# A graph-attention layer on one core: scores from f16 planes on half arrays, tiles in pair order, 46 of 48 tiles turned by DMA

## The chip, the core and the metric

The kernel runs on one core of one Trainium2 chip, in one launch. The metric is device time in microseconds, the median of the runs. TensorE (PE) multiplies; its weight loads are listed apart as PEld. VectorE (DVE), ScalarE (ACT) and GpSimd (POOL) do elementwise work. SyncE (SP) issues most transfers, and 16 DMA engines carry them out.

## The reference, cut to what matters

```
h = relu(layernorm(x))                       # x: 384 x 1024
q, k, v = h @ wq.T + bq, h @ wk.T + bk, h @ wv.T + bv
q2 = (q @ wiq.T + biq)  -> 16 heads x 384 x 64      # the same for k2 (wik), v2 (wiv)
scores = q2 @ k2.T / 8 + mask                # per head, 384 x 384
attn = softmax(scores)
out = x + (attn @ v2) @ wo.T + bo
```

The mask is -inf but for the edges of a graph (6,528 edges, softplus weights by edge type) and the diagonal. All is float32. Some biases and weights are scaled up, so that a plain f16 product is not exact enough: the kernel writes a float32 operand as a high and a low part and adds three products (high x high, high x low, low x high).

## The kernel before, in words

Weights come in 56 chunks of 128 x 1024 (`chunks`): 8 each of v, q, iv, k, then iq and ik alternately for 8 pairs of heads, then 8 of o. A chunk is loaded on SP into one of four `raw` buffers five chunks ahead (`load`, L80), and split two chunks ahead into a high part on ScalarE (`split_hi`, L102 or L108) and a low part on VectorE or GpSimd (`split_lo`, L125 and L127; in the tile loop in halves, L118, or quarters, L113). A chunk of a projection is 8 groups of three matmuls (`mm3`, L459 to L461) with 384 columns.

The iv, iq, o and k weights are scaled by a power of two and split into f16; v, q and ik stay fp32r. A scale comes from a bound: the weight chunks are read once more as "scans" (L140), ScalarE sums absolute values along each row (`scan_sum`, L146), and `bound` turns the column of row sums on TensorE (L167) and takes a maximum and a power of two (`power`, L149 to L152). There are scans for iv, k, iq and o, 8 each. The bounds are made at the chunk numbers in `BOUNDS`.

The v and q projections, the iv and the k projection fill chunks 0 to 31. Then iq and ik follow for 8 pairs of heads, from chunk 32 (`W0`) on. Their matmuls are the filler of a loop over 48 tiles: a generator gives 3 matmuls at a time (`fill_qk`), and later the output projection gives 3 matmuls of 512 columns at a time, charged 4 (`fill_o`). `PRE` = 84 of the 384 filler matmuls are done ahead of the loop, then `RATE` = 7.9 in each step. The chunks of wo are split at the steps in `WSTEPS` and released three steps later (`wready`).

A tile is 128 rows of one head's scores; before, tile i is head i // 3 and row block i % 3. `now[0]` is the step. The work of tile i stands in these steps:

- step i, `do_S` (L927, L928): two fp32r matmuls on 128 rows, since q and k of one head are stacked: rows 0 to 63 the high and 64 to 127 the low part of q, both against the high part of k; then q against a second operand (`kz`) that holds the low part of k in one half and zeros in the other. The stacks are copied together by DMA, four copies of 96 KB per operand (`qk_done`, L777), mostly on SP.
- step i + 1, `do_ttr` (L936): VectorE adds the mask and takes the row minimum (the signs are turned).
- step i + 2, `do_exp` (L941): ScalarE takes the exponential and the row sum.
- step i + 3, `do_recip` (L961, L964): reciprocals.
- 27 tiles (`in_dma`) are scaled and split into f16 planes by `do_high` (L976, ScalarE) and `do_low` (L980, VectorE) and turned by a DMA transpose on SP (`do_turn`, L984). The other 21 are scaled on GpSimd (`do_norm`, L968), turned by three fp32 transposes on TensorE (`turn_mm`, L990) and split out of PSUM by `do_pt` (L997 on ScalarE, L998 on VectorE).
- three steps after a pair's last turn, `av_mm` (L1008): 18 matmuls per pair of heads, 64 columns each, the two heads in the two halves of the columns. `do_ao` (L1013) and `do_aos` (L1016, L1017) write the result for the output projection.

The order on each queue is the order in which the loop calls these. PSUM has eight banks of 512 columns: three `g` for the filler, two `s` for scores, two `t` for transposes, one `a` for attention. At the end come the last wo chunk for six output blocks and the stores (`finish`, L877 and L1099).

Of the kernel before, what the change touches and what calls it, by code (L numbers as in the profile page):

```python
# [27 lines left out]
def gnn_kernel(ctx: ExitStack, tc: tile.TileContext, x, edges, erows, etw, wq, wk, wv, wiq, wik, wiv, wo,  # L28
# [15 lines left out]
    EB = 6  # L44
# [5 lines left out]
    def bank(tag):  # L50
        return psum.tile([128, 512], F32, tag=tag, name=tag, bufs={"g": 3, "a": 1}.get(tag, 2))
# [30 lines left out]
    def weight_scale(w):  # L82
        return {"iv": u_iv, "iq": u_iq, "o": u_o, "k": u_k}.get(chunks[w][0])
# [46 lines left out]
    SCANS = sorted([(n, i + c, i + c + g, i) for n, c, g in (("iv", 3, 2), ("k", 11, 2), ("iq", 18, 2), ("o", 25, 2)) for i in range(8)], key=lambda c: c[1])  # L130
    SROW = {"iv": 1, "k": 2, "iq": 1, "o": 2}

    def scan_buf(i):
        first = sum(c[1] < 25 for c in SCANS)
        return scan[:, i % 3, :] if i < first else qF3[:, (i - first) % 3, :]
# [6 lines left out]
    def scan_sum(w):  # L142
        for i, (n, _, at, k) in enumerate(SCANS):
            if at == w:
                x = scan_buf(i)
                nc.scalar.activation(x, x, AF.Abs, accum_out=l1[:, SROW[n], k:k + 1])  # L146

    def power(t, u, src):
        nc.vector.tensor_reduce(t, src, axis=AX.X, op=OP.max)  # L149
        nc.vector.tensor_scalar(t.bitcast(I32), t.bitcast(I32), 0x7F800000, None, op0=OP.bitwise_and)  # L150
# [3 lines left out]
    BOUNDS = {8: 0, 13: 1, 17: 2, 21: 5, 29: 3, 37: 4}  # L154

    def bound_of(w):
        return ((0, t_v, u_v), (1, t_iv, u_iv), (0, t_q, u_q), (1, t_iq, u_iq), (2, t_o, u_o), (2, t_k, u_k))[BOUNDS[w]]

    def bound_max(w):
        if w in BOUNDS:  # L160
            i, t, _ = bound_of(w)
            nc.vector.tensor_reduce(t, l1[:, i, :], axis=AX.X, op=OP.max)

    def bound(w):
        _, t, u = bound_of(w)
        ps = bank("g")
        nc.tensor.transpose(ps[:, :128], t.to_broadcast([128, 128]), ident)  # L167
        power(t, u, ps[:, :128])
# [27 lines left out]
    small = const.tile([128, 57], F32, name="small")  # L196
# [5 lines left out]
    t_k, u_k, s_k = (small[:, c:c + 1] for c in (13, 14, 15))  # L202
    l1 = const.tile([128, 3, 8], F32, name="l1")
# [132 lines left out]
    rrow = work.tile([128, 2, N], F32R, tag="qs", name="rrow").bitcast(F32)[:, 0, :]  # L336
# [21 lines left out]
    def ln_row():  # L358

        ps = bank("t")  # L360
# [13 lines left out]
    def ln_transpose(t):  # L374
        pss = []
        for half in range(2):
            ps = bank("st"[half] if t < 2 else "ga"[half])
# [108 lines left out]
    def evac_f(ps, dst, m, bias):  # L486
# [3 lines left out]
        nc.scalar.activation(f, dst[:, m, :], AF.Abs, accum_out=l1[:, 0, m:m + 1])  # L490
# [16 lines left out]
    def slot_head(w):  # L507
# [3 lines left out]
        if w > 17:  # L511
            planes_of(w - 18, qT, qF, u_q)
# [11 lines left out]
    def bounds(w):  # L524
        if w in BOUNDS:
            bound(w)
        if w == 21:
            nc.vector.tensor_scalar(s_k, t_k, 1.0 / HSC, None, op0=OP.mult)  # L528
        if w == 29:
            nc.vector.tensor_tensor(u_c, u_q, u_iq, OP.mult)  # L530
            nc.vector.tensor_scalar(bias_q, bc[:, 24:32], u_c, None, op0=OP.mult)
            nc.vector.scalar_tensor_tensor(neg_c, t_q, -0.125, t_iq, op0=OP.mult, op1=OP.mult)
# [33 lines left out]
    hk = []  # L566
    for j in range(2):
        t = work.tile([128, 2, N], F32R, tag="nat", name="hk", bufs=2).bitcast(F16)
        hk += [t.rearrange("p a n -> p (a n)").rearrange("p (k a n) -> p k a n", k=2, a=2)[:, k, :, :] for k in range(2)]
    t = work.tile([128, 2, 2, N], F32R, tag="kz", name="hkz", bufs=1).bitcast(F16)  # L570
    hk += [t.rearrange("p a b n -> p (a b n)").rearrange("p (k a n) -> p k a n", k=4, a=2)[:, k, :, :] for k in range(4)]
# [37 lines left out]
    def residual(k):  # L609

        if k == 0:
            for j in range(2):
                t = work.tile([128, 2, N], F32R, tag="ks", name="bot")
                bob[j] = t.bitcast(F32).rearrange("p k n -> p (k n)")[:, 0:512]
# [36 lines left out]
    _, vF, vT = staged("g2")  # L651
# [5 lines left out]
    accs = [bank("ststag"[i]) for i in range(6)]  # L657
# [16 lines left out]
    def v2_early():  # L674
        t = work.tile([128, 2, N], F32R, tag="qs", name="tv")
        tv = t.bitcast(F32).rearrange("p a n -> p (a n)")[:, :512]
# [24 lines left out]
    def o_scale():  # L701
        _, t, u = bound_of(W0 + 5)
# [36 lines left out]
    kz = work.tile([128, 2, 2, N], F32R, tag="kz", name="kz", bufs=1)  # L739
    for j in range(2):  # L740
        nc.gpsimd.memset(kz.bitcast(F32)[64 * j:64 * j + 64, :, 1 - j, :], 0.0)

# [3 lines left out]
    issues = []  # L746
    stacks = {}
    gps = {}

    def qk_done(w):  # L750
        n, p = chunks[w]
        q2 = nc.scalar if p == 0 else nc.sync
        if n == "iq":
            nat = work.tile([128, 2, N], F32R, tag="nat", name="nat", bufs=2)
            evac(gps[w], nat[:, 0, :], nat[:, 1, :], bias_q[:, p:p + 1])
            nf = nat.bitcast(F32)
            qs = work.tile([128, 2, N], F32R, tag="qs", name="qs")
            qf = qs.bitcast(F32)
            copies = [(nc.sync, qf[0:64, 0, :], nf[0:64, 0, :]), (q2, qf[64:128, 0, :], nf[0:64, 1, :]),
                      (nc.sync, qf[0:64, 1, :], nf[64:128, 1, :]), (q2, qf[64:128, 1, :], nf[64:128, 0, :])]  # L760
            stacks["q", p] = qs
        else:
            kh = work.tile([128, 2, N], F32R, tag="nat", name="nat", bufs=2)[:, 0, :]
            kl = kz[:, p % 2]
            evac(gps[w], kh, None, bc[:, 32 + p:33 + p])
            for o in range(2):
                r = slice(o * 64, o * 64 + 64)
                soon(1, lambda r=r, o=o, ps=gps[w]: nc.vector.scalar_tensor_tensor(  # L768
                    kl[r, o, :], ps[r, :N], bc[r, 32 + p:33 + p], kh.bitcast(F32)[r, :], op0=OP.add, op1=OP.subtract))
            nf = kh.bitcast(F32)  # L770
            ks = work.tile([128, 2, N], F32R, tag="ks", name="ks")
            kf = ks.bitcast(F32)
            copies = [(q2 if r else nc.sync, kf[r * 64:(r + 1) * 64, o, :], nf[o * 64:(o + 1) * 64, :])
                      for o in range(2) for r in range(2)]
            stacks["k", p] = ks, kl
        for q, a, b in copies:
            issue = lambda q=q, a=a, b=b: q.dma_start(a, b)  # L777
            if q is nc.scalar:
                issues.append(issue)
            else:  # L780
                after(issue)
# [13 lines left out]
    def qk_head(w):  # L795
        if pendq:
            pendq.pop(0)()
        if 0 < w - W0 < NTAB:
            mask_select(w - W0)
        split_hi(w + 2, None, False, 2 if w + 2 < WO else 1)  # L800
        while issues:
            issues.pop(0)()
# [10 lines left out]
        load(w + 5)  # L813
        scan_load(w)
        scan_sum(w)
        if w == W0:
            mask_select(0)
        if w == W0 + NTAB - 1:
            mask_scale()
        bound_max(w)  # L820
        if w == W0 + 6:
            o_scale()

    def fill_qk():
        nonlocal w
        for p in range(8):
            for n in ("iq", "ik"):
# [5 lines left out]
                for k in range(KT):  # L833
                    colmm(gps[w], w, src, k)
                    yield 3
# [9 lines left out]
    PRE, RATE, RATE_O, RATE_E = 84, 7.9, 8, 8  # L845
    WSTEPS = (35, 37, 41, 44, 47, 51)
# [72 lines left out]
    S = 48  # L919

    def do_S(i):
# [5 lines left out]
        nc.tensor.matmul(ps[:, :N], qs[:, o, c], ks[:, o, :], start=True, stop=False)  # L927
        nc.tensor.matmul(ps[:, :N], qs[:, o, c], kl[:, o, :], start=False, stop=True)  # L928

    def do_ttr(i):  # L930
        t = i % 3
        e = es[i] = work.tile([128, N], F32, tag="e", name="e", bufs=EB)
        if t == 0:
            sts[i // 3] = work.tile([128, 9], F32, tag="s", name="s", bufs=4)
        s = sts[i // 3]
        nc.vector.tensor_tensor_reduce(e, st_ps.pop(i)[:, :N], ma[:, t, :], neg_c, 3.0e38, OP.add, OP.min, s[:, t:t + 1])  # L936

    def do_exp(i):
        h, t = divmod(i, 3)
        s = sts[h]  # L940
        nc.scalar.activation(es[i], es[i], AF.Exp, bias=s[:, t:t + 1], scale=-1.0, accum_out=s[:, 3 + t:4 + t])  # L941

    ptv, plv = [], []

    XP = 1

    def pt_setup():
# [3 lines left out]
        f = ptv.pop()  # L951
        plv.extend(f[:, 2 * j:2 * j + 2, :] for j in range(3))
        plv.extend(work.tile([128, 2, N], F16, tag="pl", name="pl", bufs=XP) for _ in range(XP))

    def factor(i):
        return sts[i // 3][:, 6 + i % 3:7 + i % 3]

    def do_recip(i):
        s = sts[i // 3]
        a, b = (0, 2) if i % 3 == 1 else (2, 3)  # L960
        nc.vector.reciprocal(s[:, 6 + a:6 + b], s[:, 3 + a:3 + b])  # L961
        b = min(b, 1 + in_dma(i // 3 * 3 + 1))
        if a == 0:
# [184 lines left out]
```

## Time and profile before

| what | us |
|---|---|
| runs | 282.38 (281.54 to 287.32) |
| profiled execution, its own time | 282.02 |
| its span, first to last instruction | 280.3 |
| TensorE busy in the span | 273.9 |
| VectorE busy | 230.6 |
| ScalarE busy | 210.6 |
| first score matmul starts | 156.5 |
| last score matmul of a tile begins | 253.4 |

The span is what the trace holds; the kernel's own time is 1.7 us longer. Busy time is the union over an engine's instructions. A matmul's duration in the timeline is a latency: the next starts before it ends, so the distance between starts is what one costs TensorE.

### The profile page before, as it was taken

Reading aid. Unit: us, or ns where it says so; the run is one execution under the profiler, and the core shown is the slowest. Engines: PE = TensorE matmul, PEld = TensorE weight load, DVE = VectorE, ACT = ScalarE, POOL = GpSimd, SP = SyncE. Lnnn points to the kernel's source line nnn. Section 1 sums busy time; section 2 is a strip of 40 time slices with the busy share of each in tenths; the row PEclk is TensorE's granted clock in tenths of the full one; section 3 lists DMA queues with packets and bytes.
Section 4 is the critical chain, followed back from the end, with each engine's and each line's share of the span. In section 5 each row is a group of like instructions: output and inputs, shape, how many; then the busy total and the mean of one; then the engine's idle time right before and its main releaser. Section 6 shows DMA issues by size and latency. Waiting matters only on the chain. (4 is left out here: it accounts for less than half of the span.)

```text
span 280.3 us, 5120 instructions
## 1 busy us (share of the span) xinstructions
PE 273.9 (98%) x1631; PEld 204.0 (73%) x1631; DVE 230.6 (82%) x545; ACT 210.6 (75%) x417; POOL 146.4 (52%) x170
## 2 busy tenths in 40 slices
PE   7999999999999999999999999999999999999994
PEld 6899999999954444666677887878878695655443
DVE  4858986999998956978998987897988889999423
ACT  3796778599896927989795877688888897777510
POOL 3755656456678754659953443547373632332310
PEclk9999999999999999999999999999999999999999
DMA  7899999999987987688897699999999989432105
GB/s 254 275 303 403 383 397 381 323 302 411 348 284 258 345 289 251 238 285 321 279 329 270 173 278 257 202 199 190 213 210 197 235 218 259 108 67 48 37 12 215
DMA packets 46859, 70.42 MB, mean 251 GB/s; under 512 B 26736, under 2 KB 32368, under 8 KB 46832
## 3 DMA queue, kind: packets, MB, share of 16 engines
q1 hardware_dynamic: 44448, 67.90, 78.4%
q0 software_dynamic: 2064, 1.80, 2.4%
q10 hardware_dynamic: 320, 0.39, 0.6%
q8 instruction: 13, 0.21, 0.3%
q14 instruction: 14, 0.11, 0.1%
HBM read 55.08 MB, written 3.39 MB: 209 GB/s over the span
## 5 line engine op out<-in xcount | busy, mean ns | idle before, releaser
L459 PE MATMUL g<-g,whl 128*128 128x384 f32 (+1 forms) x248 | 83.8, 338 | 0.0
L316 POOL DMA_INDIRECT tab<-edge x51 | 61.7, 1210 | 40.8 <-DMA tab<-edge 27.2
L461 PE MATMUL g<-g,whl 128*128 128x384 f32 (+1 forms) x248 | 82.5, 333 | 0.0
L460 PE MATMUL g<-g,whl 128*128 128x384 f32 (+1 forms) x248 | 82.4, 332 | 0.0
L102 ACT ACTIVATE whl<-raw,small 128x1024 f16<-128x1024 f32 (+1 forms) x36 | 34.8, 971 | 7.9 <-DVE small L528 5.3
L125 DVE SCALAR_TENSOR_TENSOR whl<-raw,small,whl 128x1024 f16<-128x1024 f32 x24 | 32.4, 1350 | 6.4 <-ACT whl L102 6.4
L459 PEld LDWEIGHTS g<-g,whl 128*128 128x128 f32 x184 | 34.6, 188 | 0.3
L460 PEld LDWEIGHTS g<-g,whl 128*128 128x128 f32 x184 | 34.6, 188 | 0.0
L461 PEld LDWEIGHTS g<-g,whl 128*128 128x128 f32 x184 | 34.5, 188 | 0.0
L936 DVE CUSTOM_DVE_ANT_0 e<-s,ma,small 128x384 f32<-128x384 f32 x48 | 29.0, 606 | 1.7 <-PE s L928 1.4
L941 ACT ACTIVATE e<-e,s 128x384 f32<-128x384 f32 x48 | 29.1, 607 | 0.8 <-DVE s L936 0.6
L108 ACT ACTIVATE whl<-raw 128x1024 fp32r<-128x1024 f32 (+1 forms) x30 | 25.2, 848 | 1.4 <-DMA raw<-in_wv_dram 1.4
L976 ACT ACTIVATE pt<-e,s 128x384 f16<-128x384 f32 x21 | 12.9, 613 | 17.4 <-POOL s L964 17.4
L146 ACT ACTIVATE scan<-scan 128x1024 f32<-128x1024 f32 x23 | 24.0, 1044 | 0.0
L968 POOL TENSOR_TENSOR e<-e,s 128x384 f32<-128x384 f32 x21 | 17.3, 825 | 12.1 <-DVE s L961 8.2
L113 POOL TENSOR_TENSOR whl<-raw,whl 128x256 fp32r<-128x256 f32 x20 | 18.1, 912 | 8.7 <-ACT whl L108 8.7
L927 PE MATMUL s<-ks,qs 128*128 128x384 f32 x48 | 20.8, 433 | 0.7 <-DMA ks<-nat 0.3
L127 DVE TENSOR_TENSOR whl<-raw,whl 128x1024 fp32r<-128x1024 f32 x15 | 19.4, 1293 | 2.4 <-ACT whl L108 2.3
L459 PEld LDWEIGHTS <-whl 128*128 128x128 f16 x128 | 12.5, 97 | 11.0 <-issue 4.4
L1017 POOL TENSOR_TENSOR g<-aof,g 128x384 f16<-128x384 f32 x8 | 7.4, 923 | 23.8 <-ACT g L1016 23.8
L461 PEld LDWEIGHTS <-whl 128*128 128x128 f16 x128 | 12.5, 98 | 8.2
L980 DVE SCALAR_TENSOR_TENSOR pt<-e,s,pt 128x384 f16<-128x384 f32 x21 | 15.7, 749 | 3.3 <-ACT pt L976 3.3
(197 smaller groups left out, 642.7 us busy)
## 6 DMA issues: line engine op xcount, KB each, us to landing
raw<-in_wv_dram SPq DMA_DIRECT2D x8, 512.0 KB, 7.1
raw<-in_wq_dram SPq DMA_DIRECT2D x8, 512.0 KB, 6.3
scan<-in_wiv_dram SPq DMA_DIRECT2D x8, 512.0 KB, 7.2
raw<-in_wiv_dram SPq DMA_DIRECT2D x8, 512.0 KB, 5.6
scan<-in_wk_dram SPq DMA_DIRECT2D x8, 512.0 KB, 6.3
raw<-in_wk_dram SPq DMA_DIRECT2D x8, 512.0 KB, 4.7
g<-in_wo_dram SPq DMA_DIRECT2D x8, 512.0 KB, 5.8
raw<-in_wiq_dram SPq DMA_DIRECT2D x8, 512.0 KB, 4.8
```

What stands on the lines that cost most here:

```text
L102: soon(j if parts > 1 else -1, lambda c=c: nc.scalar.activation(hi[:, c], raw[w][:, c], AF.Copy, scale=sc))
L108: soon(j if parts > 1 else -1, lambda c=c: nc.scalar.activation(hi[:, c], raw[w][:, c], AF.Copy))
L125: nc.vector.scalar_tensor_tensor(lo, raw[w], sc, hi, op0=OP.mult, op1=OP.subtract)
L127: (eng or nc.vector).tensor_tensor(lo, raw[w], hi.bitcast(F32), OP.subtract)
L146: nc.scalar.activation(x, x, AF.Abs, accum_out=l1[:, SROW[n], k:k + 1])
L316: nc.gpsimd.indirect_dma_start(out=tabs[c // RNG], out_offset=bass.IndirectOffsetOnAxis(ap=idx[:, c:c + 1], axis=0), in_=val[:, c:c + 1], ...
L459: nc.tensor.matmul(ps, lhi, rhi, start=first, stop=False)
L460: nc.tensor.matmul(ps, lhi, rlo, start=False, stop=False)
L461: nc.tensor.matmul(ps, llo, rhi, start=False, stop=last)
L927: nc.tensor.matmul(ps[:, :N], qs[:, o, c], ks[:, o, :], start=True, stop=False)
L936: nc.vector.tensor_tensor_reduce(e, st_ps.pop(i)[:, :N], ma[:, t, :], neg_c, 3.0e38, OP.add, OP.min, s[:, t:t + 1])
L941: nc.scalar.activation(es[i], es[i], AF.Exp, bias=s[:, t:t + 1], scale=-1.0, accum_out=s[:, 3 + t:4 + t])
```

## The change

The iq and ik results are no longer stacked. Both are scaled to f16 planes (high and low), q by norms of the operands through the weight's own scale, k by a scale applied when it leaves PSUM. For that there are scans of ik too (40 scans in place of 32), the scans of k, iq and ik sum squares, and the scales come from square roots of the sums (`root_power`, `score_scale`). Four of the o scans are reduced on VectorE. Some scans have only one slot between load and sum, and there is a third place for their buffers.

A score tile is now three f16 matmuls (the terms high x high, low x high, high x low), each on 64 rows of the array: the even head of a pair has rows 0 to 63, the odd head rows 64 to 127. Tiles go in the order of the pairs: pair i // 6, row block, then the two heads; `do_S` does both heads in one step of two. `s` has four banks, `t` none, `a` one. All tiles but the last two are turned by DMA. The filler is paced by a planned length of a step, `STEP`, less what scores, attention and transposes are charged. `do_aos` writes its high part on VectorE. Weight loads in the loop are issued two steps later (`LD`).

```diff
-    EB = 6
+    EB = 8
...
-        return psum.tile([128, 512], F32, tag=tag, name=tag, bufs={"g": 3, "a": 1}.get(tag, 2))
+        return psum.tile([128, 512], F32, tag=tag, name=tag, bufs={"g": 3, "s": 4}.get(tag, 1))
...
-        return {"iv": u_iv, "iq": u_iq, "o": u_o, "k": u_k}.get(chunks[w][0])
+        return {"iv": u_iv, "iq": u_w, "o": u_o, "k": u_k}.get(chunks[w][0])
...
-    SCANS = sorted([(n, i + c, i + c + g, i) for n, c, g in (("iv", 3, 2), ("k", 11, 2), ("iq", 18, 2), ("o", 25, 2)) for i in range(8)], key=lambda c: c[1])
-    SROW = {"iv": 1, "k": 2, "iq": 1, "o": 2}
+    SCANS = [("iv", i + 3, i + 5, i) for i in range(8)] + [("k", i + 11, i + 13, i) for i in range(8)]
+    SCANS += [("iq", i + 16, i + 18, i) for i in range(8)]
+    SCANS += [("ik", i + 23, i + 25 - (i > 3), i) for i in range(8)] + [("o", i + 27, i + 27 + 2, i) for i in range(8)]
+    SCANS.sort(key=lambda c: c[1])
+    SROW = {"iv": 1, "k": 2, "iq": 1, "ik": 2, "o": 1}
+
+    def home(n, at):
+        return 2 if at > 24 else 1 if n == "iq" and 16 <= at < 22 else 0
...
-                nc.scalar.activation(x, x, AF.Abs, accum_out=l1[:, SROW[n], k:k + 1])
+                if n == "o" and w < 33:
+                    nc.vector.tensor_reduce(l1[:, SROW[n], k:k + 1], x, axis=AX.X, op=OP.max, apply_absolute_value=True)
+                    continue
+                nc.scalar.activation(x, x, AF.Square if n in ("k", "iq", "ik") else AF.Abs,
+                                     accum_out=l1[:, SROW[n], k:k + 1])
...
+    def root_power(t, u, src):
+        nc.vector.tensor_reduce(t, src, axis=AX.X, op=OP.add)
+        nc.vector.tensor_scalar(t.bitcast(I32), t.bitcast(I32), 1, 0x7F800000, op0=OP.logical_shift_right,
+                                op1=OP.bitwise_and)
+        nc.vector.tensor_scalar(t, t, 2.0 ** -104, 2.0 ** 50, op0=OP.max, op1=OP.mult)
+        nc.vector.reciprocal(u, t)
...
+    def bias_max():
+        ps = bank("g")
+        for i in range(3):
+            nc.tensor.transpose(ps[:, i * 128:i * 128 + 128], bmax[:, i:i + 1].to_broadcast([128, 128]), ident)
...
+    def score_scale(t, u, i, bias):
+        nc.vector.tensor_tensor(t, t, bmax[:, i:i + 1], OP.add)
+        exponent(t)
+        nc.vector.tensor_scalar(t, t, 2.0 ** -14, 2.0 ** -50, op0=OP.mult, op1=OP.max)
+        nc.vector.reciprocal(u, t)
+        nc.vector.tensor_scalar(bias, bc[:, 16 + 8 * i:24 + 8 * i], u, None, op0=OP.mult)
...
     def qk_done(w):
         n, p = chunks[w]
+        pl = qk[n, p] = work.tile([128, 2, N], F16, tag="qp" if n == "iq" else "kp", name=n, bufs=3)
+        hi, lo = pl[:, 0, :], pl[:, 1, :]
+        ps, b = gps[w][:, :N], (bias_q if n == "iq" else bias_k)[:, p:p + 1]
         if n == "iq":
...
+            nc.scalar.activation(hi, ps, AF.Identity, bias=b)
+            after(lambda: nc.vector.scalar_tensor_tensor(lo, ps, b, hi, op0=OP.add, op1=OP.subtract))
         else:
...
+            f = work.tile([128, 512], F32, tag="aof", name="f", bufs=3)[:, :N]
+            nc.scalar.activation(f, ps, AF.Identity, bias=b, scale=u_k2)
+            after(lambda: nc.vector.tensor_copy(hi, f))
+            after(lambda: (nc.gpsimd if p else nc.vector).tensor_tensor(lo, f, hi, OP.subtract))
...
-        load(w + 5)
+        soon(LD, lambda: load(w + 5))
...
-    PRE, RATE, RATE_O, RATE_E = 84, 7.9, 8, 8
-    WSTEPS = (35, 37, 41, 44, 47, 51)
+    PRE, STEP, UNIT, SMM, AMM = 90, 1.96, 0.168, 0.7, 1.69
+    WSTEPS = (36,38,41,44,47,51)
+    LD = 2
...
     def in_dma(i):
-        h, t = divmod(i, 3)
-        return t == 0 or t == 1 and (h < 10 or h == 14)
+        return i < S - 2
+
+    def tile_of(i):
+        p, r = divmod(i, 6)
+        return p, r // 2, r % 2
...
     def do_S(i):
-        h, t = divmod(i, 3)
-        p, o = divmod(h, 2)
-        qs, (ks, kl) = stacks["q", p], stacks["k", p]
-        ps = st_ps[i] = bank("s")
-        c = slice(t * 128, (t + 1) * 128)
-        nc.tensor.matmul(ps[:, :N], qs[:, o, c], ks[:, o, :], start=True, stop=False)
-        nc.tensor.matmul(ps[:, :N], qs[:, o, c], kl[:, o, :], start=False, stop=True)
+        p, t, _ = tile_of(i)
+        q, k = qk["iq", p], qk["ik", p]
+        pair = [bank("s") for _ in range(2)]
+        for j, (a, b) in enumerate(TERMS):
+            for o in range(2):
+                r = slice(o * 64, o * 64 + 64)
+                nc.tensor.matmul(pair[o][:, :N], q[r, a, t * 128:(t + 1) * 128], k[r, b, :], start=(j == 0), stop=(j == 2))
+        st_ps[i], st_ps[i + 1] = pair
...
-        nc.scalar.activation(ao[:, 0, p, :], aof[p], AF.Copy)
+        nc.vector.tensor_copy(ao[:, 0, p, :], aof[p])
...
+    LAGH, LAGL, LAGT = (5, 5), (6, 6), (6, 6)
...
+    t_at = {i + 5: i for i in range(S) if not in_dma(i)}
+    a_at = {6 * p + 14 if p < 7 else 54: p for p in range(8)}
     for i in range(S + 12):
         now[0] = i
-        r = RATE if len(gens) == 2 else RATE_O if i < S else RATE_E
+        scores = i < S and i % 2 == 0
+        r = (STEP - SMM * scores - AMM * (i in a_at) - 0.33 * (i in t_at)) / UNIT
         fill(r / 2)
-        if i < S:
+        if scores:
             do_S(i)
         fill(r / 2)
```

More of the change, by code (lines that the diff above doesn't have):

```diff
@@ L202, in gnn_kernel @@
     t_k, u_k, s_k = (small[:, c:c + 1] for c in (13, 14, 15))
+    bias_k, bmax = small[:, 57:65], small[:, 65:68]
+    t_ik, u_ik, t_q2, u_q2, t_k2, u_k2, u_q7, u_w = (small[:, c:c + 1] for c in range(68, 76))
     l1 = const.tile([128, 3, 8], F32, name="l1")
@@ L335, in gnn_kernel @@
     var = lnt[:, 1:2 * NT:2]
[L336 removed]
+    rrow = work.tile([128, N], F32, tag="qp", name="rrow", bufs=3)
     def ln_bn(t, h):
@@ L376, in ln_transpose @@
         for half in range(2):
-            ps = bank("st"[half] if t < 2 else "ga"[half])
+            ps = bank("s" if t < 2 else "ga"[half])
             for j in range(4):
@@ L564, in proj @@
             w += 1
[L566 to L571, printed above, removed]
+    hk = [work.tile([128, 2, N], F16, tag="pl" if k < 5 else "kp", name="hk", bufs=5 if k < 5 else 3)
+          for k in range(KT)]
     hs = {}
@@ L655, in gnn_kernel @@
     proj(hT, qF, 0, extra_q)
-    accs = [bank("ststag"[i]) for i in range(6)]
+    accs = [bank("ssssag"[i]) for i in range(6)]
     for k in range(8):
@@ L674, in v2_early @@
     def v2_early():
-        t = work.tile([128, 2, N], F32R, tag="qs", name="tv")
-        tv = t.bitcast(F32).rearrange("p a n -> p (a n)")[:, :512]
+        tv = work.tile([128, 512], F32, tag="aof", name="tv", bufs=3)
         nc.scalar.activation(tv, accs[5], AF.Copy)
@@ L738, in gnn_kernel @@
     flush(True)
-    kz = work.tile([128, 2, 2, N], F32R, tag="kz", name="kz", bufs=1)
-    for j in range(2):
-        nc.gpsimd.memset(kz.bitcast(F32)[64 * j:64 * j + 64, :, 1 - j, :], 0.0)
     ao = gtile("g1").bitcast(F16).rearrange("p a k n -> p (a k n)")[:, :2 * KT * N]
     ao = ao.rearrange("p (a k n) -> p a k n", a=2, k=KT)
-    issues = []
-    stacks = {}
+    qk = {}
     gps = {}
@@ L834, in fill_qk @@
                     colmm(gps[w], w, src, k)
+                    if k == 5 and w == W0 + 1:
+                        bounds(w)
                     yield 3
@@ L1082, in gnn_kernel @@
             f()
-        for x in at(TURN, i):
-            do_turn(x)
+        for o in range(2):
+            x = i - LAGT[o]
+            if x % 2 == o and 0 <= x < S and in_dma(x):
+                do_turn(x)
         if i in WSTEPS:
```

206 lines of the change are left out of this document (92 added, 114 removed).

## The prediction, made before the result was known

> **What bounds the kernel now.** I read the page first, then the windows view, then TensorE's timeline.
>
> ```profile
> span 280.3 us, 5120 instructions
> PE 273.9 (98%) x1631; PEld 204.0 (73%) x1631; DVE 230.6 (82%) x545; ACT 210.6 (75%) x417; POOL 146.4 (52%) x170
> ```
>
> ```profile
> 140.00:160.00 20.00, 20.00 (x121) 15.54 (x119) 18.68 (x24) 15.30 (x29) 8.69 (x7) 1.00 0.77 262
> 160.00:180.00 20.00, 19.61 (x117) 16.01 (x115) 16.80 (x48) 14.55 (x37) 8.35 (x12) 1.00 1.00 246
> 180.00:200.00 20.00, 20.00 (x137) 14.67 (x138) 17.75 (x43) 17.15 (x42) 11.01 (x15) 1.00 0.94 196
> 200.00:220.00 20.00, 19.70 (x129) 16.07 (x129) 17.52 (x42) 16.68 (x43) 11.89 (x15) 1.00 0.97 219
> 220.00:240.00 20.00, 20.00 (x136) 14.24 (x133) 17.84 (x45) 16.55 (x37) 7.57 (x13) 1.00 0.91 225
> 240.00:260.00 20.00, 20.00 (x125) 11.28 (x123) 18.33 (x42) 15.02 (x36) 6.52 (x11) 1.00 0.32 66
> ```
>
> In the windows the columns behind the length are PE, PEld, DVE, ACT and POOL busy time, then the granted clock, the DMA share and GB/s. From 140 to 260 us TensorE is idle 0.39 + 0.30 = 0.7 us, at the full clock. So the time is the sum of TensorE's issue slots, and a change pays what it takes out of that sum, less the holes it makes. The durations on the page are latencies of overlapped matmuls; the slot is the distance between starts.
>
> ```profile
> 186.43 0.33 PE L461 MATMUL g<-g,whl 128*128 128x384 f16 x1
> 186.59 0.33 PE L459 MATMUL g<-g,whl 128*128 128x384 f16 x1
> ...
> 203.33 0.33 PE L927 MATMUL s<-ks,qs 128*128 128x384 f32 x1
> 203.50 0.33 PE L928 MATMUL s<-kz,qs 128*128 128x384 f32 x1
> 203.67 0.33 PE L459 MATMUL g<-g,whl 128*128 128x384 f32 x1
> 203.85 0.33 PE L460 MATMUL g<-g,whl 128*128 128x384 f32 x1
> ```
>
> ```profile
> 263.22 0.38 PE L461 MATMUL g<-g,g 128*128 128x512 f16 x1
> 263.44 0.49 PE L990 MATMUL t<-ident,e 128*128 128x128 f32 x3
> 263.77 0.38 PE L459 MATMUL s<-g,g 128*128 128x512 f16 x1
> ...
> 266.14 0.38 PE L461 MATMUL g<-g,g 128*128 128x512 f16 x1
> 266.45 1.65 PE L1008 MATMUL a<-pt,vhl 128*64 128x384 f16 x18
> 268.04 0.39 PE L459 MATMUL g<-g,g 128*128 128x512 f16 x1
> 268.26 0.38 PE L460 MATMUL g<-g,g 128*128 128x512 f16 x1
> ```
>
> The first pair gives 0.16 us for a 384-column f16 matmul, the last pair of that fence 0.18 (0.17 on the mean) for fp32r. The two score matmuls of a tile take 203.67 - 203.33 = 0.34. A tile's three transposes take 0.33. The 18 attention matmuls take 1.59, 0.088 each: they are 64 columns wide, and two run side by side in the halves of the array, since one alone takes 0.16. Ahead of them 266.45 - 266.14 - 0.22 = 0.10 us is lost (0.22 is the 512-column slot, 268.26 - 268.04), behind them nothing.
>
> **The change, part by part.**
>
> Scores. Before: 48 tiles of about 0.35 us (0.34 above, a little more beside f16 work): 16.8 us. After: 24 pairs of six f16 matmuls, each on 64 of the array's rows, two heads alternating. No row of this trace shows matmuls on half of the rows. Bounds: as fast as the attention's halves, 6 x 0.088 + 0.10 = 0.63 us a pair, or one after the other, 6 x 0.16 + 0.10 = 1.06. I take 0.63, because the attention rows are the nearest thing: two groups with separate weights, rows of their own here, and PSUM banks of their own. 24 x 0.63 = 15.2 us, so -1.6 us; the other end is +8.6. The Trainium skill (TensorEngine Tiling, Key Properties) says that a change of tiling mode drains TensorE. The 0.10 us ahead of the attention group agrees, and with 24 new groups such drains would cost 24 x 0.10 = 2.4 us, which the 0.63 holds.
>
> Transposes. Before, 21 tiles of 48 are turned on TensorE (21 x 0.33 = 6.9 us); after, 2 (0.7). -6.3 us, rounded up by the code's three per tile. This is the main term.
>
> Bounds. One bound more and three bias maxima are four transposes of a column at about 0.11 us: +0.4.
>
> Idle time. The score matmul waited for the stack copies and the attention for a turn; the copies go. Of the 0.7 us I take 0.5 back. The sum so far is 282.0 - 1.6 - 6.3 + 0.4 - 0.5 = 274.0, made against the profiled execution's own 282.0 us (span 280.3), which lies 0.4 below the runs' median of 282.38.
>
> The cover. TensorE's saving counts only if nothing else becomes the bound, so here are the others' accounts.
>
> ```profile
> L936 DVE CUSTOM_DVE_ANT_0 e<-s,ma,small 128x384 f32<-128x384 f32 x48 | 29.0, 606 | 1.7 <-PE s L928 1.4 <-POOL g L1017 0.2
> L768 DVE SCALAR_TENSOR_TENSOR kz<-g,bc,nat 64x384 fp32r<-64x384 f32 x16 | 9.7, 608 | 1.4 <-ACT nat L469 1.2
> L998 DVE SCALAR_TENSOR_TENSOR pt<-t,pt 128x384 f16<-128x384 f32 x21 | 11.2, 551 | 1.9 <-ACT pt L997 1.7
> L980 DVE SCALAR_TENSOR_TENSOR pl<-e,s,pl 128x384 f16<-128x384 f32 x6 | 3.7, 609 | 0.0
> L583 DVE CAST hkz<-hs 128x384 f16<-128x384 f32 x4 | 1.6, 399 | 0.0
> L125 DVE SCALAR_TENSOR_TENSOR whl<-raw,small,whl 128x1024 f16<-128x1024 f32 x24 | 32.4, 1350 | 6.4 <-ACT whl L102 6.4
> L976 ACT ACTIVATE pl<-e,s 128x384 f16<-128x384 f32 x6 | 3.6, 605 | 2.1 <-POOL s L964 2.1
> L997 ACT ACTIVATE pt<-t 128x384 f16<-128x384 f32 x21 | 9.5, 473 | 1.5 <-PE t L990 1.5
> L1016 ACT ACTIVATE g<-aof 128x384 f16<-128x384 f32 x8 | 4.2, 520 | 0.1
> L146 ACT ACTIVATE g<-g 128x1024 f32<-128x1024 f32 x9 | 9.4, 1047 | 3.7 <-issue 3.7
> L681 DVE TENSOR_REDUCE small<-t 128x1 f32<-128x512 f32 x2 | 1.4, 682 | 0.0
> ```
>
> VectorE in the tile loop: the two half-height low planes of k go (-9.7); 19 low planes out of PSUM become low planes out of SBUF (19 x (0.609 - 0.551) = +1.1); eight casts of k and eight of the attention output at 0.40 come (+6.4): -2.2 against the 88.2 us that the five rows from 160 to 260 add up to. ScalarE: 19 x (0.605 - 0.473) = +2.5, eight copies of the output go (-4.2): -1.7 against 79.9. The loop loses about 8 of these 100 us, so VectorE has 86.0 us of work in 92 (93%) and ScalarE 78.2 (85%), where they had 88% and 80%. The cover is thin but holds.
>
> Scans. Eight more weight tiles are read to form the ik norm. ScalarE sums four more (40 less 4 on VectorE, where it had 32), 4 x 1.05 = 4.2 us, and VectorE reduces four at about 1.4 (an estimate: twice the 0.68 of 512 columns). All of this lies ahead of the loop, beside TensorE work that is unbroken there. VectorE is 93% busy from 140 to 160, but the mask's selects and scaling move one weight slot later, a bound's small operations move to an earlier slot, and ScalarE's 3.7 us of waiting for its own stack-copy issues goes. Some ik scans are summed one slot after their load and not two, with this landing time:
>
> ```profile
> scan<-in_wk_dram SPq DMA_DIRECT2D x8, 512.0 KB, 6.3
> ks<-nat SPq DMA_DIRECT2D x30, 96.0 KB, 4.0
> pt<-pt SPq DMA_TRANSPOSE x21, 3.5
> ```
>
> A slot of 24 matmuls at 0.16 is 3.9 us, so ScalarE can wait 6.3 - 3.9 = 2.4 us there. The weight halves are made two slots ahead, which hides it. Between 0 and +3 us; I take +0.5, together with the tail and single late attention groups, since the rows show no hole on TensorE in this stage now.
>
> SP's queue and the DMA engines.
>
> ```profile
> 175.63 1.22 SPq L984 DMA_TRANSPOSE pt<-pl  x1
> 178.14 2.41 SPq L777 DMA_DIRECT2D qs<-nat  x4
> ```
>
> A turn holds SP 1.22 us, a stack copy 2.41 / 4 = 0.60. SP gains 19 turns (+23 us) and loses 60 copies (-36 us), so it has more room, and one turn per step of 1.96 us fits. A pair's last turn is issued in step 6p + 11, its attention stands in step 6p + 14: three to four steps, 5.9 to 7.8 us, against 3.5 from issue to landing. Hidden.
>
> The lull. This is the one hole that I can count. The filler has 16 x 24 = 384 matmuls of iq and ik, 90 of them ahead of the loop. With 1.96 us a step, 0.7 charged for every second step and 1.69 for an attention group, at 0.168 a matmul, a step without attention gets 9.6 matmuls and six steps with one 47. The remaining 294 end in step 35, where the old rate of 7.9 and 300 last to step 38. Then six output groups stand ready, which last to step 37, while the third weight chunk is released at 39 and the fourth at 41. Steps 37 to 40 hold two score pairs, one attention group and two output groups, 4.4 us of TensorE work. VectorE has four score tiles at 0.61, four low planes at 0.61, two weight halves at 1.35 and a cast in them: 8.0 us. TensorE loses 3.6 us if it cannot run ahead and next to nothing if it can run two pairs ahead. The four score banks let it run about half that far: +2.0.
>
> **Sum:** 274.0 + 0.5 + 2.0 = **276.5 us**, 2.1% under the median.
>
> **The rivals.**
>
> No hole (the lull is covered by TensorE running ahead): 274.0. For it: TensorE is idle 0.7 us in 120 now. Against it: the count above.
>
> VectorE as bound: if it gets no more than the 88% that it reached before, its 86.0 us take 97.7 where TensorE needs 92, +5.7 on 274.0: 279.7. For it: 18.33 of 20 in the last row is the highest share shown in the loop. Against it: that row is from a stage in which TensorE had no hole either.
>
> Heads one after the other on the row halves: +8.6 for -1.6 makes 286.7, less about 2 of holes which the longer matmuls cover (then the 2.5 of holes is hardly seen): 284.7 by 274.0 + 10.2 + 0.5. This one ends slower than before; it decides from a pair of about 0.87 us on, where 24 pairs take back the other 4 us. Against it: the attention rows.
>
> Late turns: 46 turns, one a step, with loads in the same queue. From about 7 us to landing each attention group waits; at 8.5 us seven groups lose about 2 each: 290. Against it: 3.5 us at landing, at a DMA share of 0.91 to 1.00 already. The Trainium skill (VectorE: DVE Perf Modes, The three transpose paths) puts a 128x128 bf16 block at 1309 ns by DMA and 390 ns on TensorE and advises TensorE; by it the six blocks of a tile would take 7.9 us by DMA, and 46 of them far more than the loop. The trace has 1.22 us of issue and 3.5 to landing for all six blocks, so here it does not agree.
>
> **How the numbers follow.** About 2% (276.7 against 288.0) is what a measurement of this kernel can tell from no change. Likeliest case 60%, 274.5 to 280, of which 34 below 276.7; no hole 14%; VectorE as bound 11%; heads in series 9%, of which 2 above 288; late turns 6%. Faster 34 + 14 = 0.48; slower 2 + 6 = 0.08; same 0.44. The range runs from 272.0 (no hole, and the pair a little cheaper) to 284.7, which leaves out the late turns and the upper part of the series case.
>
> **What would show it.** Six score matmuls of a pair spaced near 0.09 us, not 0.16; six transposes on TensorE in place of 63; no wait of scores on a DMA; a TensorE hole of about 2 us near the change from iq/ik filler to output filler; turns landing within 5 us. The prediction falls if score matmuls space at 0.16, or if TensorE's idle time in the loop exceeds 6 us.

## The result and the profile after

The changed kernel takes 278.97 us in the median, the kernel before 282.03 in the same comparison. The ratio is 0.990, with a 95% interval of 0.988 to 0.992: about 3 us faster, which is less than the 2% that counts as a clear difference here, and 2.5 us slower than the 276.5 forecast. Its profiled execution takes 279.5 us. Two of its 20 runs, 282.0 and 282.1 us, stand more than 1.5% above its fastest at a mean granted clock of 0.99; the medians here and below include such runs.

The first lines of the page and two stretches of the windows view of the kernel after. The columns behind the length are PE, PEld, DVE, ACT and POOL busy time, granted clock, DMA share, GB/s.

```profile
span 277.4 us, 5039 instructions
PE 268.0 (97%) x1626; PEld 186.9 (67%) x1626; DVE 235.0 (85%) x565; ACT 215.1 (78%) x417; POOL 141.3 (51%) x163
```

```profile
140.00:160.00 20.00, 18.86 (x113) 14.38 (x111) 18.48 (x29) 11.69 (x21) 8.77 (x6) 1.00 0.96 366
160.00:260.00 100.00, 98.05 (x653) 57.90 (x652) 91.25 (x222) 87.35 (x199) 42.52 (x59) 1.00 0.84 174
```

TensorE is busy 268.0 us where it was busy 273.9, so 5.9 us less; the span is only 2.9 us shorter. In these 120 us TensorE now stands idle 1.14 + 1.95 = 3.1 us, where it was 0.7. VectorE is busy 91% of the last 100 us, near the 93% that was worked out ahead.

TensorE's timeline of the kernel after, first around two score groups (one between f16 matmuls, one between fp32r matmuls):

```profile
163.88 0.33 PE L495 MATMUL g<-g,whl 128*128 128x384 f16 x1
164.04 0.33 PE L496 MATMUL g<-g,whl 128*128 128x384 f16 x1
164.30 0.66 PE L957 MATMUL s<-ik,iq 64*128 64x384 f16 x6
164.89 0.34 PE L494 MATMUL g<-g,whl 128*128 128x384 f16 x1
165.06 0.33 PE L495 MATMUL g<-g,whl 128*128 128x384 f16 x1
...
168.31 0.34 PE L496 MATMUL g<-g,whl 128*128 128x384 f32 x1
168.58 0.66 PE L957 MATMUL s<-ik,iq 64*128 64x384 f16 x6
169.17 0.44 PE L494 MATMUL g<-g,whl 128*128 128x384 f32 x1
169.45 0.33 PE L495 MATMUL g<-g,whl 128*128 128x384 f32 x1
```

```profile
L957 PE MATMUL s<-ik,iq x144: 322/323/333, 160.2 to 250.0; 64*128 64x384 f16 x144
```

The second fence is the line's own view; its three times are the least, the median and the longest latency of one. The group is busy 0.66 us and its last matmul is in flight 0.32, so the last one starts 0.34 after the first: two slots of 0.17. The six matmuls go in three rounds of two, as the same timeline shows when its window ends inside the group (at 164.45 and at 164.48):

```profile
164.30 0.34 PE L957 MATMUL s<-ik,iq 64*128 64x384 f16 x2
164.30 0.50 PE L957 MATMUL s<-ik,iq 64*128 64x384 f16 x4
```

The next ordinary matmul starts at 0.59, so 0.25 after the last round and not 0.16; and the group begins 0.26 after the start of the matmul ahead of it and not 0.16. So a pair costs 3 x 0.163 of work, 0.10 to enter the half-array mode and 0.10 to leave it: 0.69 us, and not the 0.63 forecast. Where fp32r follows, the next slot is 169.45 - 169.17 = 0.28 instead of 0.17, about 0.1 more.

Six of the 24 pairs run straight into an attention group:

```profile
245.14 0.38 PE L496 MATMUL g<-whl,g 128*128 128x512 f16 x1
245.45 0.66 PE L957 MATMUL s<-ik,iq 64*128 64x384 f16 x6
246.04 1.65 PE L1029 MATMUL a<-pt,vhl 128*64 128x384 f16 x18
247.63 0.39 PE L494 MATMUL g<-whl,g 128*128 128x512 f16 x1
```

From 245.14 to 247.63, less a 512-column slot of 0.22, both groups take 2.27 us. An attention group by itself takes 0.10 + 1.59 = 1.69 in the kernel before, so the pair adds 0.58 here and not 0.69: one change of mode serves both.

Then the two places where TensorE stood still longest after the first microseconds, at the ik bound and in the output filler, with ScalarE's row behind the first one:

```profile
149.24 0.34 PE L496 MATMUL g<-g,whl 128*128 128x384 f32 x1
150.44 0.29 PE L187 MATMUL g<-ident,small 128*128 128x128 f32 x1 [0.86 <-DVE small L182]
...
237.65 0.39 PE L494 MATMUL g<-whl,g 128*128 128x512 f16 x1
239.69 0.38 PE L495 MATMUL g<-whl,g 128*128 128x512 f16 x1 [1.65 <-DVE whl L125]
```

```profile
141.60 0.67 ACT L761 ACTIVATE vhl<-s,small 128x512 f16<-128x512 f32 x1
145.48 1.06 ACT L155 ACTIVATE g<-g 128x1024 f32<-128x1024 f32 x1 [3.20 <-DMA g<-in_wik_dram]
```

```profile
149.02 1.21 DVE L153 TENSOR_REDUCE l<-g 128x1 f32<-128x1024 f32 x1
150.15 0.15 DVE L182 TENSOR_REDUCE small<-l 128x1 f32<-128x8 f32 x1
```

ScalarE waits 3.2 us for the last ik scan. The k projection's results that stand behind it on ScalarE come late, VectorE's low parts of them come late, and the reduction of the eight ik sums (L182) stands behind them and behind one more o scan (L153) on VectorE. TensorE reaches the bound's transpose and waits. At 238 us TensorE has the high part of a wo chunk and waits for VectorE's low part.

### The profile page after: what moved, and what is told of

Read it like the earlier page. It is cut to its first block, busy times and chain, and to the rows that moved or that the text cites. A ratio compares the mean times of both kernels' runs of the same rounds, so it can differ in the third digit from the quotient of the medians.

```text
span 277.4 us, 5039 instructions
## 1 busy us (share of the span) xinstructions
PE 268.0 (97%) x1626; PEld 186.9 (67%) x1626; DVE 235.0 (85%) x565; ACT 215.1 (78%) x417; POOL 141.3 (51%) x163
## 4 chain that ended last, share of the span: by engine, by line
PE 76%; DVE 10%; DMA 5%; ACT 4%; issue 3%; SPq 0%; POOL 0%; DVEq 0%; ACTq 0%; POOLq 0%
PE g L494 19%; PE g L496 18%; PE g L495 18%; PE s L957 4%; PE a L1029 4%; PE s L494 3%; PE s L495 3%; PE s L496 3%; DVE whl L125 3%; DMA g<-in_wik_dram 3%; DMA g<-in_x_dram 2%; PE g L595 2%; DVE ma L364 2%; ACT e L971 1%; DVE l L153 1%
## 5 line engine op out<-in xcount | busy, mean ns | idle before, releaser
L125 DVE SCALAR_TENSOR_TENSOR whl<-raw,small,whl 128x1024 f16<-128x1024 f32 x24 | 34.3, 1430 | 4.0 <-ACT whl L102 3.7
L1005 DVE SCALAR_TENSOR_TENSOR pl<-e,s,pl 128x384 f16<-128x384 f32 x46 | 32.0, 696 | 5.9 <-ACT pl L1001 5.7
L1001 ACT ACTIVATE pl<-e,s 128x384 f16<-128x384 f32 x46 | 27.7, 605 | 3.2 <-POOL s L987 3.1
L987 POOL TENSOR_SCALAR s<-s 128x2 f32<-128x2 f32 x23 | 8.7, 380 | 38.8 <-DVE s L985 38.8
L155 ACT ACTIVATE g<-g 128x1024 f32<-128x1024 f32 x16 | 16.7, 1047 | 6.0 <-DMA g<-in_wik_dram 4.2
L155 ACT ACTIVATE scan<-scan 128x1024 f32<-128x1024 f32 x20 | 20.9, 1044 | 0.0
L494 PE MATMUL g<-hk,whl 128*128 128x384 f16 x64 | 20.9, 326 | 0.0
L495 PE MATMUL g<-hk,whl 128*128 128x384 f16 x64 | 20.9, 326 | 0.0
L496 PE MATMUL g<-hk,whl 128*128 128x384 f16 x64 | 20.9, 326 | 0.0
L113 POOL TENSOR_TENSOR whl<-raw,whl 128x256 fp32r<-128x256 f32 x20 | 16.3, 824 | 6.9 <-ACT whl L108 5.1
```

Of the source, the lines that this page charges most:

```text
L125: nc.vector.scalar_tensor_tensor(lo, raw[w], sc, hi, op0=OP.mult, op1=OP.subtract)
L155: nc.scalar.activation(x, x, AF.Square if n in ("k", "iq", "ik") else AF.Abs, accum_out=l1[:, SROW[n], k:k + 1])
L494: nc.tensor.matmul(ps, lhi, rhi, start=first, stop=False)
L495: nc.tensor.matmul(ps, lhi, rlo, start=False, stop=False)
L496: nc.tensor.matmul(ps, llo, rhi, start=False, stop=last)
L1001: nc.scalar.activation(planes[i][:, 0, :], es[i], AF.Copy, scale=factor(i))
```

## The experiments

Ratios are to the kernel before, run on the same chip, with the 95% interval. "Now" is the changed kernel at 0.990.

**Do two heads run side by side, and is it the order that does it?**

```diff
-        for j, (a, b) in enumerate(TERMS):
-            for o in range(2):
+        for o in range(2):
+            for j, (a, b) in enumerate(TERMS):
```

> The changed kernel with the six score matmuls of a pair in another order: three of the even head, then three of the odd head, in place of the two heads by turns. Theory (two neighbours on different row halves run side by side): the group grows from 0.59 us to 6 x 0.16 = 0.98, 24 groups cost 9.4 us more, of which some 1 to 2 fill holes that are there now: 286 to 288 us. Rival (a matmul on 64 rows is simply that short, about 0.1 us, whatever stands beside it): no change, 279.

Measured 278.84 us, 0.986 (0.983 to 0.989): no clear change, so the number that the theory gave was wrong. The rival's number is right, but not its reason, as the trace and the next run show:

```profile
165.24 0.67 PE L957 MATMUL s<-ik,iq 64*128 64x384 f16 x6
165.84 0.34 PE L494 MATMUL g<-g,whl 128*128 128x384 f16 x1
```

0.67 us of busy time with a last latency of 0.32 again put the last start two slots after the first, although the three matmuls of one head were issued ahead of the three of the other. Here too the first two of the six start together (a window that ends at 165.41 shows two in 0.34 us). So TensorE itself runs the two row halves side by side. The Trainium skill (TensorEngine Tiling, Key Properties) says that tiles work independently and that different tiles can load weights and multiply in parallel; the trace agrees (0.67 us for six). To tell the theories apart the halves themselves must be taken away:

```diff
-                r = slice(o * 64, o * 64 + 64)
+                r = slice(0, 64)
```

> The changed kernel with both heads' score matmuls on rows 0 to 63 (the odd head then uses the even head's operands; the output isn't the reference's). Theory (two matmuls run side by side only because they stand on different halves of the rows): the starts of the six become 0.16 us apart, the group grows from 0.59 us to about 1.08, 24 x 0.49 = 11.8 us more less up to 3 in holes: 287 to 291 us. Rival (a 64-row matmul is half as long by itself): 279.

Measured 288.73 us, 1.024 (1.022 to 1.026), about 9.8 us more than now.

```profile
165.17 1.15 PE L957 MATMUL s<-ik,iq 64*128 64x384 f16 x6
166.25 0.34 PE L494 MATMUL g<-g,whl 128*128 128x384 f16 x1
```

The last start is now 1.15 - 0.32 = 0.83 after the first, five slots of 0.166 (the granted clock is 1.00 in the 20 us from 160 on). On one half a 64-row matmul takes a whole slot; two run together only on different halves. The next matmul starts 1.08 after the group's start; with 0.10 on the way in, a pair costs 1.18. The forecast's rival "heads one after the other" had put such a pair at 1.06 and the kernel at 284.7; forced, it came out 4 us slower than that, on the slower side as that rival said.

**Is it slots or the change of mode?** On the best version (below) each group was issued twice.

```diff
-        for j, (a, b) in enumerate(TERMS):
+        for j, (a, b) in list(enumerate(TERMS)) * 2:
```

> The kernel with later o scans and earlier wo chunks (276.05 us), each pair's six score matmuls issued twice into the same banks, the second pass writing the same values again. Theory (a group is rounds of two matmuls, 0.163 us each, and a fixed 0.20 us to enter and leave the half-array mode): three rounds more, 24 x 0.49 = 11.7 us, less the 0.9 us hole, 286.8. Rival (0.59 us is six equal slots of 0.098 and the mode change is free): 24 x 0.59 = 14.2, 289.3 or more.

Measured 287.0 us, 1.015 (1.008 to 1.022).

```profile
162.15 1.15 PE L957 MATMUL s<-ik,iq 64*128 64x384 f16 x12
163.23 0.34 PE L494 MATMUL g<-g,whl 128*128 128x384 f16 x1
```

Twelve matmuls have their last start at 0.83, six rounds, and the next matmul follows at 1.08 where it followed at 0.59: 0.49 for three rounds. In all they cost 10.9 us, 0.46 a group, so the other 0.2 us of the 0.69 is fixed. That agrees with rounds and a fixed price, and not with 0.098 for each matmul (14.2).

**Are the removed transposes the gain?** Eight more tiles were given back to TensorE.

```diff
     def in_dma(i):
-        return i < S - 2
+        return i < S - 2 and i % 12 > 1
```

> The changed kernel with 8 more tiles (row block 0 of every second pair of heads) turned on TensorE, 10 in place of 2. Theory (a tile turned on TensorE costs it 0.33 us and up to 0.11 more for going back to fp32r): 8 x 0.33 to 8 x 0.44, 281.6 to 282.5. Rival (TensorE isn't the bound in the loop of the changed kernel): 279.

Measured 282.91 us, 1.003 (0.998 to 1.008): 3.9 us more than now by the medians. That difference is soft: the five runs lie between 280.0 and 285.4, and the profiled one (280.0) has no hole at the ik bound, where the changed kernel's has one. The profile of the run with later o scans (276.5, below) has no such hole either. Between these two, whose first 20 us differ by 0.2 us of TensorE's time, lie 3.5 us, 0.44 a tile: about 1 us of it is waits, and 2.5 us, 0.31 a tile, is slots. The transposes of a tile take the expected 0.32 (171.52 to 171.84), and the first of a pair can wait for GpSimd's scaling:

```profile
169.46 0.55 PE L1014 MATMUL s<-ident,e 128*128 128x128 f32 x3 [0.74 <-POOL e L991]
...
171.52 0.49 PE L1014 MATMUL s<-ident,e 128*128 128x128 f32 x3
171.84 0.33 PE L494 MATMUL g<-g,whl 128*128 128x384 f16 x1
```

So turning tiles by DMA carries the gain, and 8 tiles back use up about all of it.

**Then why not that alone?** The kernel before, with its stacks, and 46 tiles turned by DMA.

```diff
     def in_dma(i):
...
-        return t == 0 or t == 1 and (h < 10 or h == 14)
+        return i < S - 2
...
-    HIGH, LOW, TURN = (4, 4), (5, 5), (5, 5)
+    HIGH, LOW, TURN = (4, 4, 4), (5, 5, 5), (5, 5, 5)
...
```

> The kernel before with its stacks and tile order, but 46 of 48 tiles turned by DMA. Theory (the removed transposes are the gain, 57 x 0.11 = 6.3 us of TensorE time, and nothing stands against it but SP): if SP has room, 276. Rival (the stack copies had to go first): SP needs 46 x 1.22 + 60 x 0.60 + about 20 loads x 0.5 = 102 us where the loop has 97, so turns come late and attention groups wait: 283 to 290.

Measured 294.23 us, 1.044 (1.040 to 1.049): 12 us slower. TensorE's three longest waits in the loop, one row of its timeline each:

```profile
184.24 2.05 PE L1010 MATMUL a<-pt,vhl 128*64 128x384 f16 x17 [3.49 <-DMA pt<-pt]
...
228.61 1.79 PE L1010 MATMUL a<-pt,vhl 128*64 128x384 f16 x16 [2.97 <-DMA pt<-pl]
...
254.63 0.41 PE L927 MATMUL s<-ks,qs 128*128 128x384 f32 x1 [2.40 <-DMA ks<-nat]
```

Attention groups wait for turns and scores for stacks, both from SP's queue, as the count of its issue time (102 us in a loop of 97) said. The buffers of this version are those of the kernel before, so they could be short too. But in SP's own timeline the rows of issued transfers fill 95 of the 100 us from 156 to 256, where they fill 85 in the kernel before and 80 in the changed one: the queue is all but full. The waits also cost more than their length. After the 3.49 us wait the filler's f16 matmuls start 0.32 apart for a while, not 0.16, and the granted clock is 0.83 from 180 to 190 us; after the 2.97 us wait it is 0.85 from 230 to 240. By these clocks the two stretches lose 1.7 and 1.5 us of the 12, an estimate. The f16 planes pay nothing on TensorE, but they empty the queue that the turns need.

**Where did the rest go: the scans.** Without the loads and sums of the ik scans (k's scale is then made from other sums):

```diff
-            if at == w:
+            if at == w and n != "ik":
                 nc.sync.dma_start(scan_buf(i), W[n][k])
...
-            if at == w:
+            if at == w and n != "ik":
                 x = scan_buf(i)
```

> The changed kernel without the loads and the sums of the ik scans; the ik bound is made from the sums that the k scans left, so k's scale is another one. Theory (ScalarE's waits for ik scans, 4.2 us in all, push VectorE's work back, and TensorE waits for it at the ik bound, 1.4 us between 149 and 152): these waits go, 277.3, and the first scores start 1.5 us earlier. Rival (the bound's own chain of small operations or the mask selects delay TensorE): less than 0.5 us, 278.6 or more.

Measured 276.86 us, 0.984 (0.981 to 0.987), and TensorE is busy 20.00 of the 20 us from 140 to 160. So the ik scans hold about 2 us. The next run keeps all scans and moves those of o:

```diff
-    SCANS += [("ik", i + 23, i + 25 - (i > 3), i) for i in range(8)] + [("o", i + 27, i + 27 + 2, i) for i in range(8)]
+    SCANS += [("ik", i + 23, i + 25 - (i > 3), i) for i in range(8)] + [("o", i + 30, i + 32, i) for i in range(8)]
...
-                if n == "o" and w < 33:
+                if n == "o" and w < 30:
...
-                27: (1, t_iq, u_iq, 1), 33: (2, t_ik, u_ik, 1), 38: (1, t_o, u_o, 0)}.get(w)
+                27: (1, t_iq, u_iq, 1), 33: (2, t_ik, u_ik, 1), 41: (1, t_o, u_o, 0)}.get(w)
...
-        _, t, u, _ = bound_of(W0 + 6)
+        _, t, u, _ = bound_of(W0 + 9)
...
-        if w == W0 + 7:
+        if w == W0 + 10:
             o_scale()
```

> The changed kernel with all its scans, but those of o loaded at chunks 30 to 37 in place of 27 to 34, summed two chunks later, all eight on ScalarE, and the o bound and scale made three chunks later. Theory (the wait at the ik bound comes from ik and o scans that share three buffers and one queue): ScalarE's waits for ik scans and TensorE's hole at the ik bound go, and so does most of the spread between runs: 277.3, against 276.9 without the ik scans at all. Rival (it is the eight more loads themselves, 4.2 MB, that fill the DMA engines): 279.

Measured 276.5 us, 0.980 (0.978 to 0.983).

```profile
140.00:160.00 20.00, 20.00 (x123) 15.01 (x122) 18.73 (x28) 14.55 (x28) 8.97 (x6) 1.00 0.83 309
```

The hole at the ik bound is gone with all 40 scans in place, and ScalarE waits for no ik scan any more. So it isn't the 4.2 MB by themselves but the company: ik and o scans in three buffers on one queue, with one slot between load and sum. One thing isn't separated: this edit also takes the four reductions of o scans (L153, 1.2 us each) off VectorE ahead of the bound. They can't make the hole alone, since the run without ik scans still has them and has no hole. The five runs also lie closer together, 275.7 to 277.2 where the 20 of the changed kernel lie between 277.2 and 282.1.

How long TensorE stands at this bound differs from profile to profile. Its starts lie 1.20 us apart there in the changed kernel's, 2.60 with the heads in series, and 2.84 in a profiled execution of 284.3 us (the first run of the next section):

```profile
151.00 0.34 PE L496 MATMUL g<-g,whl 128*128 128x384 f32 x1
153.84 0.29 PE L187 MATMUL g<-ident,small 128*128 128x128 f32 x1 [2.50 <-DVE small L182]
...
156.15 0.53 PE L496 MATMUL g<-g,whl 128*128 128x384 f16 x1
156.47 0.53 PE L494 MATMUL g<-g,whl 128*128 128x384 f16 x1
```

Soon after these 2.84 us matmuls start 0.32 apart, twice the usual distance, until 157.75, and the granted clock of the 20 us from 140 on is 0.91. After the 2.60 it stayed at 1.00. So a hole of nearly 3 us at this place costs more than itself. That this makes most of the spread of the runs is likely but not shown, since only one execution of each kernel was profiled.

**The lull.** Four runs moved the wo chunks' split steps (36 and 38 in the changed kernel) or the filler ahead of the loop.

```diff
-    WSTEPS = (36,38,41,44,47,51)
+    WSTEPS = (34, 36, 41, 44, 47, 51)
```

> The changed kernel with the third and fourth chunk of wo split at steps 34 and 36 in place of 36 and 38. Theory (TensorE's 1.65 us hole at 238 us comes from the output filler running dry before these chunks are released): the hole goes, 277.3. Rival (VectorE is the bound in these steps and the hole only moves): 279, with the same idle time elsewhere between 225 and 245 us.

Measured 279.7 us, 0.990 (0.986 to 0.993): no gain that can be told. The hole near 238 us is gone from its profile, but the holes ahead of the loop (1.57 and 2.50 us) hide such a gain, so the rest was run with the later o scans. Steps 35 and 37:

> The same with the third and fourth wo chunk split one step earlier (35 and 37). Theory of the lull (the filler runs dry until these chunks are released): 0.8 to 1.6 us of the hole near 239 us goes beside the scans' part: 275.9. Rival (VectorE is the bound in these steps, the hole moves to an attention group): 277.3.

Measured 276.05 us, 0.980 (0.978 to 0.981), the lowest median of all; its difference from 276.5 is inside the intervals. The hole in the profile shrank from 1.64 to 0.93. The same with `PRE` at 84 in place of 90:

> The same kernel (276.05 us) with 84 in place of 90 filler matmuls ahead of the loop. Theory of the lull (the filler of the loop runs dry before the third and fourth wo chunk): it lasts 0.6 of a step longer, the 0.9 us hole goes: 275.2. Rival (scores that start 1 us earlier only wait for VectorE's mask work): 276 or a little more.

Measured 276.32 us, 0.977 (0.972 to 0.983). The hole stays at 0.93:

```profile
235.66 0.38 PE L495 MATMUL g<-whl,g 128*128 128x512 f16 x1 [0.93 <-DVE whl L125]
```

Six filler matmuls more in the loop leave it as long, so it isn't the filler running dry that sets its length. Steps 34 and 36 with the later o scans:

> The kernel with later o scans (276.5 us), third and fourth wo chunk split at steps 34 and 36. Theory now (the hole of 1.65 us is TensorE waiting for VectorE to make the low part of a wo chunk, whenever that stands in VectorE's queue; one step earlier left 0.93): two steps earlier the hole near 235 us is gone and nothing replaces it: 275.2. Rival (VectorE has no time to give in these steps; its later work, a turn's low plane, is late in its place and an attention group waits): a hole of about 1 us on an attention group, 276.

Measured 276.25 us, 0.979 (0.975 to 0.983). The hole near 235 us is gone, but the time is the same, and there are new waits at the end, the larger on the last attention group:

```profile
259.03 0.39 PE L496 MATMUL g<-g,g 128*128 128x512 f16 x1 [0.23 <-POOL g L1038]
260.57 1.76 PE L1029 MATMUL a<-pt,vhl 128*64 128x384 f16 x14 [0.53 <-DVE pt L1021]
```

These come to 0.76 us where the hole was 0.93. Our reading, not tested by itself: output filler that is done early is missing in the tail, where it covered the last tiles' way through VectorE. The lull is then a loan, repaid in large part at the end; closing it is worth less than can be measured here.

## Why the prediction was right, and where it was not

The direction, the range and the likeliest mechanism hold; the size is half of the forecast. And that it misses by no more than 2.5 us is in part luck, since the terms' errors go both ways.

- Transposes, -6.3: right. Six are left of 63, and eight tiles given back cost 3.5 us between two profiles without a hole at the bound, 2.5 of it in slots, where 2.6 to 3.5 was expected.
- Scores, -1.6: this term was mis-sized. "Behind them nothing" was the wrong step. The attention's 18 matmuls in the profile of before are busy 1.65 us with a latency of 0.33, so the last round starts at 1.32, eight slots of 0.165, and the next matmul 0.27 after it. The 0.088 that I divided out holds 0.10 for leaving the mode, spread over nine rounds; over three rounds it weighs three times as much. A pair costs 0.69, 24 pairs 16.6. Six pairs share a change of mode with an attention group (-0.6), and going back to fp32r costs about 0.1 in nine places, five behind scores and four behind such an attention group (+0.9): 16.9 against 16.8. The rewrite of the scores gains TensorE nothing, where 1.6 us was forecast.
- Mode change: the forecast weighed it with 24 x 0.10; the runs show it twice per group, 24 x 0.20 = 4.8 us, or 4.2 with the six that are shared.
- The scans, "+0.5 together with the tail": too low by 1.6 to 2.0. They are worth 2.1 to 2.5 us (without ik, or with o moved). The forecast did see that ScalarE can wait some 2.4 us there (it waited up to 3.2), but took the two slots of lead for enough. The work that came too late was not a weight half but VectorE's reduction for the bound (L182).
- The lull, +2.0: the hole is there (1.65 us), but its cause as counted is not: TensorE waits for VectorE's low part of a chunk, and 6 filler matmuls more left the hole of the later runs as long. Closing it gained at most 0.45 us, inside the intervals. So this term was too high by 1.5 to 2.0, and it stood in for what the scans cost.
- Together: scores +1.7, scans +1.6 to 2.0 and lull -1.5 to -2.0 give 1.3 to 2.2 of the 2.5 us that the forecast missed; no run shows where the rest lies.
- Idle time, -0.5, and the column transposes, +0.4: TensorE waits for no stack any more; neither term was tested alone.
- SP: right. It has room for the turns once the copies are gone (rows for 80 us in 100), and with both it has not (95).
- The rivals: heads in series did not come, and the run that forced it cost 9.8 us for the 10.2 counted; that is close by offsetting errors, since a pair takes 1.18 and not 1.06 and its price starts from 0.69 and not 0.63. VectorE as bound at 88% did not come either: it went to 91%, and TensorE waited for it for 0.27 and 1.65 us in the loop. Late turns did not come: no attention group waits for one.

What stays open: TensorE's first 20 us differ by up to 2.2 us of busy time between the profiled executions (17.9 in that of the kernel before, 17.1 in the changed kernel's, 18.6 in the best version's, 16.4 to 18.6 over all). Whole single profiles can't be compared to better than that, and 0.8 of the 5.9 us that TensorE is less busy lies there; the verdicts here rest on the timed runs.

## What to carry to other kernels

A mode of the array has a price at each end, so cost a group by its first and last start and the next ordinary start, and not by its mean: six half-array matmuls in three rounds cost 0.69 us where the mean of a long group promised 0.53. What a change frees on a queue can be worth more than what it saves on the engine: here the f16 planes pay nothing on TensorE but make room for 19 DMA turns, which carry the gain. A hole in the bounding engine is not worth its length: closing the one in the output filler gained nothing that can be measured, closing the one at the ik bound gained 2.5 us, more than its 1.1 us in the profile. So try closing a hole before counting it.

## What the runs showed of the hardware beyond that

Two matmuls on different row halves run side by side whatever order they are issued in (0.67 us of busy time for six, issued three and three), and on the same half they do not (1.15). The mode change costs 0.10 us on the way in and 0.10 on the way out, and a score group and an attention group in a row share one (2.27 us together, where apart they take 0.69 and 1.69). A VectorE split of 128x1024 (L125) takes 1.28 us in the median of 24. Three took 1.83, 2.34 and 3.05 us, and each of them overlaps an addition on GpSimd (L666). That the addition is the cause wasn't tested. The longest of them:

```profile
128.41 3.05 DVE L125 SCALAR_TENSOR_TENSOR whl<-raw,small,whl 128x1024 f16<-128x1024 f32 x1
...
129.08 1.29 POOL L666 TENSOR_TENSOR res<-res,bot 128x512 f32<-128x512 f32 x1
```
